# A softplus logarithm beside attention: from ScalarE's table to an eighteen-step polynomial on GpSimd

## The chip, the cores and the metric

The program runs on one core of a Trainium2 chip. The core has five instruction queues that run in order, each by itself: TensorE (PE in the profile; its weight loads are PEld), VectorE (DVE), ScalarE (ACT), GpSimd (POOL) and SyncE (SP, which here only issues DMAs). An instruction that waits for another engine holds up everything behind it in its own queue. The metric is device time in microseconds (us), the median of several executions; the profile is one further execution.

## The reference, cut to what matters

x has shape (4, 1024, 256) in float32: 4 batches of 1024 rows, 8 tiles of 128 rows each. One layer of three parts:

```python
x = x + attn_a(layernorm(x))      # 16 heads of 16, full softmax over 1024 keys, plus its own residual
x = x + ffn(layernorm(x))         # one 256x256 ternary weight
x = x + attn_b(layernorm(x))      # the memory: a recurrent fast-weight layer over the rows
x = x + ffn(layernorm(x))
```

The change lies in attn_b, in one of its three gates:

```python
alpha = (sigmoid(hidden @ aW.T + ab) * 0.1).mean(-1)
eta   = (sigmoid(hidden @ eW.T + eb) * 0.9 + 0.05).mean(-1)
theta = (softplus(hidden @ tW.T + tb) * 0.1).mean(-1)      # one number per row
```

For every chunk of 128 rows theta scales the gradient step of the fast weights; the chunks follow one another.

## The kernel before

**Attention.** The queries are cut into four blocks of 256 rows (BLOCKS, numbered k from 0 to 3). A unit is one block, one batch and half of the heads: 32 units. A unit runs over 8 tiles of keys and two pairs of heads, so 16 half-steps. A half-step (half) has TensorE compute the maxima scores of a later unit (mx, L244), the scores of this one (sc, L284 and L292) and, later, the weighted values (av, L312); VectorE reduces the maxima (nm, L249) and ScalarE takes the exponential of the scores (pt, L298, two instructions of 128x512 in a half-step). The scores live in three PSUM buffers.

**What runs beside it.** When a block's attention is through for a batch, finish (two row tiles at a time) adds the output projection, normalizes (hn), runs the feed-forward part, normalizes again (hd), transposes, and keeps hidden@tW.T+tb in xs. When a block is complete for all four batches, two calls of theta start, one for each chunk of 128 rows: chunks 0 and 1 in block 0, 2 and 3 in block 1, 4 and 5 in block 2, 6 and 7 in block 3. Then the memory of the chunk runs (prepare, advance, retrieve, output). Blocks 0 to 2 have their theta and memory beside the attention of the block that follows. Block 3 has no attention behind it: its chunks 6 and 7 are the tail, from about 1345 us on.

**theta before.** With x the 128x256 tile of xs (L505 to L515): VectorE makes u = min(-x, x); ScalarE u = exp(u) (L507); VectorE w = 1 + u (L509) and the rounding error u = (w - 1) - u (L510); ScalarE w = ln(w) (L512); GpSimd w = w - u (L513); VectorE w = max(x, 0) + w (L515). TensorE then takes the mean over the 64 features (thp, L521) and VectorE writes theta (thn, L525), which advance uses at L748. The exponential of the attention and the tanh of the memory share one of ScalarE's tables, the logarithm needs another one: the profile shows an ACT_TABLE_LOAD before the logarithm and one at the next exponential or tanh.

**The order.** The queues of PE, DVE and ACT are written out by hand, those of POOL and SP follow the order in which the program is recorded. A small planner interleaves the generators: each lane (settle, finish, theta, memory, outputs and so on) holds generators; "yield 1" means that the next piece of this generator comes no earlier than 1 unit of planner time later; a half-step is half a unit and the pieces' own TensorE work counts too (half, beside, piece). So a step of theta that changes its yields moves the pieces that come after it in all queues. The planner knows nothing of the time that POOL takes.

**POOL's other work.** The inverse square roots of all normalizations are a power on POOL: rsqrt (L72), then two small instructions in norm_stats (L84, L85) that make the bias; ScalarE applies them (L91, 128x256 for each row tile). In advance, the norm of the gradient goes through POOL too (n, L733), then wt on DVE (L748). prepare has several POOL copies and products (ms L591, xl L663, s1e to s2a L743, kl L548, qq L654).

```python
A.activation(dst[i], src[i], AF.Identity, scale=r[:, i : i + 1], bias=nb[:, i : i + 1])   # L91, hn and hd
```

Of the kernel before, what the change touches and what calls it, by code (L numbers as in the profile page):

```python
# [12 lines left out]
AF = mybir.ActivationFunctionType  # L13
ALU = mybir.AluOpType
# [12 lines left out]
D = 64  # L27
N5 = 512
EPS_LN = 1e-5

OWN = {mybir.EngineType.PE, mybir.EngineType.DVE, mybir.EngineType.Activation}


BLOCKS = ((0, 256), (256, 256), (512, 256), (768, 256))
# [3 lines left out]
def tile_hybrid(ctx: ExitStack, tc: tile.TileContext, x, ln_gamma, ln_beta, w_qkv, b_qkv, w_out, b_out,  # L38
# [3 lines left out]
    V, G, A = nc.vector, nc.gpsimd, nc.scalar  # L42
# [24 lines left out]
    def rsqrt(src, n, scale, eps, name):  # L67

        t = small.tile([P, 8], F32, tag="rs_in", name=f"rsi_{name}")
        r = small.tile([P, 8], F32, tag="rs_out", name=f"rso_{name}")  # L70
        V.tensor_scalar(t[:, :n], src, float(scale), float(eps), ALU.mult, ALU.add)  # L71
        G.tensor_tensor(out=r[:, :n], in0=t[:, :n], in1=nhalf[:, :n], op=ALU.pow)  # L72
        return r

    def norm_stats(src, n, name):
# [3 lines left out]
        for i in range(n):  # L79
            V.bn_stats(st[:, i, :], src[i])  # L80
            V.bn_aggr(mv[:, i, :], st[:, i, :])
        r = rsqrt(mv[:, :n, 1], n, 1.0, EPS_LN, name)
        nb = small.tile([P, 4], F32, tag="ln_nb", name=f"nb_{name}")
# [83 lines left out]
    def mps(shape, name, columns=256):  # L167

        taken[0] += columns
        return pools["m"].tile(shape, F32, tag="m", name=name)  # L170
# [325 lines left out]
    def theta(k, cs):  # L496


        xh = xs_of[k][:, cs].rearrange("p c b t -> p (c b t)")
        m = cs.stop - cs.start  # L500
        u, w = (
            pools["lp"].tile([P, N5 // 2], F32, tag=f"th{name}", name=f"{name}_{k}_{cs.start}")[:, : 2 * m * P]
            for name in "uw"
        )
        V.scalar_tensor_tensor(out=u, in0=xh, scalar=-1.0, in1=xh, op0=ALU.mult, op1=ALU.min)  # L505
        yield 1
        A.activation(u, u, AF.Exp)  # L507
        yield 1
        V.tensor_scalar(w, u, 1.0, None, ALU.add)  # L509
        V.scalar_tensor_tensor(out=u, in0=w, scalar=-1.0, in1=u, op0=ALU.add, op1=ALU.subtract)  # L510
        yield 1
        A.activation(w, w, AF.Ln)  # L512
        G.tensor_sub(w, w, u)  # L513
        yield 1
        V.scalar_tensor_tensor(out=w, in0=xh, scalar=0.0, in1=w, op0=ALU.max, op1=ALU.add)  # L515
        yield 2
        ps = mps([P, m, 2, 2], f"thp_{k}_{cs.start}", 256)
        for c in range(m):
            for b in range(2):
                o = (2 * c + b) * P  # L520
                T.matmul(ps[:, c, :, b], lhsT=w[:, o : o + P], rhs=ot, start=True, stop=True)  # L521


        c0 = BLOCKS[k][0] // P + cs.start
        V.tensor_scalar(thn[:, c0 : c0 + m, :], ps.rearrange("p c h b -> p c (h b)"), -0.01, None, ALU.mult)  # L525
        yield 1
# [466 lines left out]
    with ExitStack() as by_hand:  # L993
        by_hand.enter_context(tc.manual_schedule(engines=OWN))
        share(m=8)
        with ExitStack() as s1_:
# [105 lines left out]
            def input_stats(b):  # L1102
# [9 lines left out]

                V.tensor_scalar(r[:, 0, :], mv[:, :, 1], EPS_LN, None, ALU.add)
                G.tensor_tensor(out=r[:, 1, :], in0=r[:, 0, :], in1=nhalf, op=ALU.pow)
                G.tensor_mul(r[:, 2, :], r[:, 1, :], r[:, 1, :])
                G.tensor_mul(r[:, 2, :], r[:, 2, :], mv[:, :, 1])
                G.tensor_scalar(r[:, 2, :], r[:, 2, :], EPS_LN, None, ALU.add)
                G.tensor_tensor(out=r[:, 3, :], in0=r[:, 2, :], in1=nhalf, op=ALU.pow)
# [84 lines left out]
            def thetas(k, cs):  # L1203
                yield from theta(k, cs)
                for c in range(NT)[BLOCKS[k][0] // P :][cs]:
                    got[c]["theta"] = True
# [248 lines left out]
```

## Time and profile before

| what | value |
|---|---|
| median of 3 executions | 1477.69 us (1477.01 to 1477.88) |
| the profiled execution: time, span | 1477.84 us, 1476.1 us |
| granted TensorE clock, mean over the span | 0.929 |
| PE, DVE, ACT, POOL busy over the span | 92%, 69%, 53%, 16% |
| attention and what runs beside it, 250 to 1345 us | PE busy 1045.4 of 1095 us, clock 0.96 |
| tail, 1345 to 1476.1 us | PE busy 96.7 of 131.1 us, clock 0.78 |

How to read it: the page gives busy shares of the whole span; the table by stages cuts the span into windows; the timeline lists instructions in order of time, with the idle time of their engine ahead of them and what ended it in brackets. A name such as w<-w,u is output and inputs. The time outside the span (1.74 us in the profiled execution) is start and end.

### The profile page before, as it was taken

How to read it: one execution, taken by the hardware profiler on the slowest of the kernel's cores; microseconds unless marked ns; L12 is line 12 of the kernel's file. 1: busy time of each engine (PE TensorE's matmuls, PEld its weight loads, DVE VectorE, ACT ScalarE, POOL GpSimd, SP SyncE). 2: the span in 40 equal slices, each digit the busy share in tenths (PEclk: the TensorE clock that was granted, in tenths of full speed). 3: DMA queues.
4: the chain of work that ended last, by engine and by line, in shares of the span. 5: the costliest groups of instructions: out<-in, count | busy, mean ns of one | idle time of the engine just before them, and what ended most of it. 6: DMA issues, size and time to landing. Idle time of an engine off the chain costs nothing. (4 is left out here: it accounts for less than half of the span.)

```text
span 1476.1 us, 32993 instructions
## 1 busy us (share of the span) xinstructions
PE 1356.1 (92%) x13568; PEld 843.4 (57%) x13568; DVE 1020.5 (69%) x1640; ACT 785.9 (53%) x1477; POOL 236.8 (16%) x432
## 2 busy tenths in 40 slices
PE   6589999999999999999998999999999999996886
PEld 4346555556555556565654565666556656664664
DVE  5766767587777766877778767776778677712653
ACT  2124636466666555656566655655665555553333
POOL 4431111000000200211011101210102102201232
PEclk9759989999999789999999999999999899988877
DMA  6605432533333221222233222223232022101000
GB/s 219 203 32 197 142 135 81 199 103 109 106 101 112 81 60 59 65 76 84 90 101 109 76 84 77 86 77 98 77 126 80 17 76 90 49 23 37 22 8 29
DMA packets 98211, 132.71 MB, mean 90 GB/s; under 512 B 27980, under 2 KB 70284, under 8 KB 98060
## 3 DMA queue, kind: packets, MB, share of 16 engines
q1 hardware_dynamic: 97788, 129.81, 27.6%
q8 instruction: 107, 1.75, 0.5%
q10 hardware_dynamic: 272, 0.79, 0.1%
q14 instruction: 44, 0.36, 0.1%
HBM read 89.69 MB, written 38.76 MB: 87 GB/s over the span
## 5 line engine op out<-in xcount | busy, mean ns | idle before, releaser
L298 ACT ACTIVATE pt<-sc 128x512 f32<-128x512 f32 x1024 | 555.2, 594 | 452.2 <-PE sc L292 451.6
L249 DVE TENSOR_REDUCE nm<-mx 128x2 f32<-128x1024 f32 x512 | 617.8, 1220 | 144.1 <-PE mx L244 126.1
L284 PE MATMUL sc<-q0slot,kslot 32*128 32x256 f32 x2048 | 373.4, 339 | 24.2 <-ACT pt L298 12.8
L312 PE MATMUL av<-pt,v 128*32 128x256 f32 x4096 | 310.6, 404 | 6.9 <-DVE a L320 6.2
L284 PE MATMUL sc<-q1slot,kslot 32*128 32x256 f32 x2048 | 309.7, 291 | 0.0
L244 PE MATMUL mx<-kslot,q0slot 32*128 32x512 f32 x1024 | 264.8, 516 | 24.3 <-DVE lo L1160 14.0
L284 PEld LDWEIGHTS sc<-q0slot,kslot 32*128 32x128 f32 x2048 | 239.1, 191 | 51.0 <-ACT pt L298 25.4
L244 PEld LDWEIGHTS mx<-kslot,q0slot 32*128 32x128 f32 x1024 | 98.2, 189 | 241.0 <-issue 117.2
L292 PE MATMUL sc<-mslot,ones_r 32*128 32x512 f32 x1024 | 232.5, 405 | 1.8 <-DMA mslot<-d 1.8
L284 PEld LDWEIGHTS sc<-q1slot,kslot 32*128 32x128 f32 x2048 | 233.8, 193 | 0.0
L244 PE MATMUL mx<-kslot,q1slot 32*128 32x512 f32 x1024 | 217.0, 422 | 0.0
L312 PEld LDWEIGHTS av<-pt,v 128*32 128x32 f32 x4096 | 99.2, 111 | 126.9 <-issue 88.8
L292 PEld LDWEIGHTS sc<-mslot,ones_r 32*128 32x128 f32 x1024 | 124.1, 193 | 2.5 <-DMA mslot<-d 2.4
L244 PEld LDWEIGHTS mx<-kslot,q1slot 32*128 32x128 f32 x1024 | 101.2, 195 | 0.0
L1155 PE MATMUL cps<-hT,wg 128*128 128x512 f32 x128 | 61.4, 626 | 0.0
L1160 DVE SCALAR_TENSOR_TENSOR lo<-cps,bqk,hi 128x512 fp32r<-128x512 f32 x32 | 23.9, 751 | 53.4 <-ACT hi L1159 45.4
L1159 ACT ACTIVATE hi<-cps,bqk 128x512 fp32r<-128x512 f32 x32 | 22.0, 687 | 49.9 <-PE cps L1155 24.8
L72 POOL TENSOR_TENSOR rso_hn<-rsi_hn,nhalf 128x2 f32<-128x2 f32 (+1 forms) x17 | 12.0, 708 | 223.1 <-DVE rsi_hn L71 196.8
L72 POOL TENSOR_TENSOR rso_hd<-rsi_hd,nhalf 128x2 f32<-128x2 f32 (+1 forms) x17 | 12.0, 703 | 187.4 <-DVE rsi_hd L71 170.1
L893 PE MATMUL opf<-ffn,ohT 128*128 128x256 f32 x128 | 35.1, 422 | 6.6 <-ACT ohT L888 6.6
L1155 PEld LDWEIGHTS cps<-hT,wg 128*128 128x128 f32 x128 | 24.3, 200 | 28.8 <-issue 26.6
L1196 POOL TENSOR_SCALAR X<-X,rr_a 128x256 f32<-128x256 f32 x32 | 18.5, 588 | 124.4 <-DVE h L1138 124.4
(361 smaller groups left out, 1662.4 us busy)
## 6 DMA issues: line engine op xcount, KB each, us to landing
kslot<-dk SPq DMA_DIRECT2D x64, 512.0 KB
v<-dv SPq DMA_DIRECT2D x32, 604.0 KB
q1slot<-dq SPq DMA_DIRECT2D x128, 64.0 KB
q0slot<-dq SPq DMA_DIRECT2D x64, 128.0 KB
da<-a SPq DMA_DIRECT2D x31, 256.0 KB
dv<-vtile SPq DMA_DIRECT2D x8, 604.0 KB
X<-in_L_attn_a_x_dram SPq DMA_DIRECT2D x8, 512.0 KB
dq<-hi SPq DMA_DIRECT2D x16, 256.0 KB
```

The lines of the kernel that those rows point to most:

```text
L72: G.tensor_tensor(out=r[:, :n], in0=t[:, :n], in1=nhalf[:, :n], op=ALU.pow)
L244: T.matmul(ps[:, e, :], lhsT=qS[u][p][o : o + SL, j * P : (j + 1) * P], rhs=kt[o : o + SL, hf * N5 : (hf + 1) * N5], start=p == 0, stop=p ...
L249: V.tensor_reduce(nms[u][:, hf, 2 * pr : 2 * pr + 2, j], ps, AX.X, ALU.max, negate=True)
L284: T.matmul(ps[e][:, g * w : (g + 1) * w], lhsT=kS[u, g][o : o + SL, kc * P : (kc + 1) * P], rhs=qS[u][p][o : o + SL, g * w : (g + 1) * w], ...
L292: T.matmul(ps[e], lhsT=ones[o : o + SL, :], rhs=mslots[u % 2][o : o + SL, :], start=False, stop=True, skip_group_check=True,)
L298: A.activation(pt[:, e, :], ps[e], AF.Exp, scale=1.0 / HD**0.5)
L312: T.matmul(avs[u][SL * i : SL * (i + 1), part * w : (part + 1) * w], lhsT=v[:, kc, o : o + SL], rhs=pts[u, kc, i // 2][:, i % 2, part * w ...
L893: T.matmul(pf[:, e, :], lhsT=hT[:, cc, e, :], rhs=ffn[:, cc, :], start=cc == 0, stop=cc == 1)
L1155: T.matmul(ps, lhsT=wg[:, cc, n * P : (n + 1) * P], rhs=hT[:, cc, o], start=cc == 0, stop=cc == 1)
L1159: A.activation(high, ps, AF.Identity, bias=bqk[:, n : n + 1])
L1160: V.scalar_tensor_tensor(out=low, in0=ps, scalar=bqk[:, n : n + 1], in1=high.bitcast(F32), op0=ALU.add, op1=ALU.subtract,)
L1196: G.tensor_scalar(Xt, Xt, r[:, 6, t : t + 1], r[:, 7, t : t + 1], ALU.mult, ALU.add)
```

## The change

For blocks 0 to 2 (chunks 0 to 5) softplus' ln(1 + u), with u = exp(-|x|) between 0 and 1, is computed on POOL as a polynomial of degree 10 without a constant term, by Horner's rule, in eighteen instructions of 128x256. The two DVE instructions that split 1 + u, ScalarE's logarithm and POOL's subtraction go. The yields change with it: two pauses of 0.5 inside the polynomial and 1 after it. Block 3, whose theta lies in the tail, keeps the logarithm.

```diff
+LOG1P = (
+    1.0, -0.49999904, 0.33330004, -0.24954559, 0.19678117, -0.15311863, 0.10614265, -0.0570642, 0.01990716, -0.00325638
+)
@@ theta
         A.activation(u, u, AF.Exp)
         yield 1
-        V.tensor_scalar(w, u, 1.0, None, ALU.add)
-        V.scalar_tensor_tensor(out=u, in0=w, scalar=-1.0, in1=u, op0=ALU.add, op1=ALU.subtract)
-        yield 1
-        A.activation(w, w, AF.Ln)
-        G.tensor_sub(w, w, u)
-        yield 1
+        if k == len(BLOCKS) - 1:
+            V.tensor_scalar(w, u, 1.0, None, ALU.add)
+            V.scalar_tensor_tensor(out=u, in0=w, scalar=-1.0, in1=u, op0=ALU.add, op1=ALU.subtract)
+            yield 1
+            A.activation(w, w, AF.Ln)
+            G.tensor_sub(w, w, u)
+            yield 1
+        else:
+            G.tensor_scalar(w, u, LOG1P[-1], LOG1P[-2], ALU.mult, ALU.add)
+            for n, c in enumerate(LOG1P[-3::-1]):
+                G.tensor_mul(w, w, u)
+                G.tensor_scalar(w, w, c, None, ALU.add)
+                if n % 3 == 2:
+                    yield 0.5
+            G.tensor_mul(w, w, u)
+            yield 1
         V.scalar_tensor_tensor(out=w, in0=xh, scalar=0.0, in1=w, op0=ALU.max, op1=ALU.add)
```

In the order that results, POOL has the eighteen instructions in one stretch, but for two instructions of prepare (ms and the carry copy) in chunks 0, 2 and 4, and the power n of advance in the middle of chunks 3 and 5. From chunk 2 on the planner also sets the pieces of theta, memory and output at other half-steps than before on PE, DVE and ACT.

## The prediction

> **What bounds the kernel now.** First the table by stages, then half-clock stretches of it (columns: window; its length, then busy us and count of PE, PEld, DVE, ACT, POOL; granted clock; DMA share; GB/s).
>
> ```profile
> 250.00:1345.00 1095.00, 1045.39 (x11468) 649.40 (x11468) 782.73 (x1159) 649.75 (x1227) 130.72 (x249) 0.96 0.27 85
> ...
> 484.20:497.90 13.70, 13.65 (x115) 7.12 (x115) 11.06 (x21) 6.87 (x12) 3.72 (x9) 0.50 0.11 21
> ...
> 538.90:542.30 3.40, 3.40 (x32) 1.55 (x30) 3.33 (x9) 1.65 (x5) 0.53 (x1) 0.50 0.04 7
> ...
> 846.10:849.50 3.40, 3.40 (x27) 1.88 (x26) 2.44 (x6) 1.67 (x3) 0.65 (x2) 0.50 0.00 1
> ```
>
> Beside the attention PE is busy for 95%: it is the bound, and every us in which it idles is lost. The other three rows are the second loss: half clock, with PE fully busy. Then the groups by form, for what POOL pays (count | busy us, mean ns | idle before):
>
> ```profile
> L1196 POOL TENSOR_SCALAR X<-X,rr_a 128x256 f32<-128x256 f32 x32 | 18.5, 588 | 124.4 <-DVE h L1138 124.4
> ...
> L513 POOL TENSOR_TENSOR w<-w,u 128x256 f32<-128x256 f32 x8 | 5.9, 738 | 51.3 <-ACT w L512 51.3
> ```
>
> Third, ACT's timeline around the logarithm of chunk 1 (start, us; brackets: idle before):
>
> ```profile
> 517.47 0.42 ACT L507 ACTIVATE u<-u 128x256 f32<-128x256 f32 x1
> ...
> 528.82 1.09 ACT L91 ACTIVATE hd<-X,nb_hd,rso_hd 128x256 f32<-128x256 f32 x2
> ...
> 531.95 1.08 ACT L298 ACTIVATE pt<-sc 128x512 f32<-128x512 f32 x2 [0.51 <-PE sc L292]
> 533.05 1.28 ACT L512 ACT_TABLE_LOAD   x1
> 534.35 0.42 ACT L512 ACTIVATE w<-w 128x256 f32<-128x256 f32 x1
> 534.67 0.83 ACT L725 ACTIVATE sq<-dra 128x768 f32<-128x768 f32 x1
> 535.52 1.28 ACT L298 ACT_TABLE_LOAD   x1
> 536.81 1.09 ACT L298 ACTIVATE pt<-sc 128x512 f32<-128x512 f32 x2
> ```
>
> and the two engines on either side of it:
>
> ```profile
> 527.16 0.73 POOL L72 TENSOR_TENSOR rso_hd<-rsi_hd,nhalf 128x2 f32<-128x2 f32 x1 [14.05 <-DVE rsi_hd L71]
> 527.97 0.20 POOL L84 TENSOR_TENSOR nb_hd<-mv_hd,rso_hd 128x2 f32<-128x2 f32 x1
> 528.25 0.23 POOL L85 TENSOR_SCALAR nb_hd<-nb_hd 128x2 f32<-128x2 f32 x1
> ```
>
> ```profile
> 537.46 0.38 PE L284 MATMUL sc<-q0slot,kslot 32*128 32x256 f32 x1 [1.99 <-ACT pt L298]
> ```
>
> The reader is to see two things. The logarithm's two loads and itself (2.98 us) made pt 3.26 us late (536.81 against 533.55 by the 1.60 us spacing just before), and PE idled for 1.99 of them: 1.27 us of lateness are absorbed. And between u's exponential (517.89) and the normalization hd, which waits for POOL, lie four half-steps.
>
> **What goes.** PE's idle time that ended with the ACT row behind a logarithm: 1.24 us (chunk 0, at 484.25), 1.99 (1, at 537.46), 1.24 + 0.48 (2, at 796.28 and 799.16), 1.99 (3, at 845.42), 1.24 + 0.48 (4, at 1106.95 and 1109.83), 0.29 (5, at 1149.91): 8.95 us. Behind three of them the clock halves: 13.7, 3.4, 3.4 us. At half clock pt follows pt every 2.60 us (489.44 to 492.04), at full clock every 1.60 (800.10 to 801.70), so 38% of such a stretch is lost: 5.3 + 1.3 + 1.3 = 7.9 us. Bounds: 0, if these stretches have other causes, and 15.8, if the 6.8 us from 808.5 and the 13.7 us from 1146.4 belong here too; I take 7.9, the three that begin within 2 us of the idle. ACT's own 6 x 2.98 us and DVE's 6 x 0.73 us (L509, L510) are worth nothing beyond this: both engines have idle time in the half-steps (ACT 0.51 us in the row at 531.95).
>
> **What comes.** Eighteen POOL instructions in a chain: nine like L1196 (0.59), nine like L513 (0.74); a dependent one follows after 0.09 us (527.16 + 0.73 to 527.97: 0.08): 9 x 0.68 + 9 x 0.83 = 13.5 us. POOL is idle enough (131 of 1095 us), but its queue is in order.
>
> Chunks 0, 2, 4: behind the polynomial stand only prepare's xl and s1e to s2a, and DVE's L515. From exponential to L515 there were 19.6, 18.3 and 18.3 us; less 3 us for the logarithm that is gone, 15.3 remain, against 13.5 and 0.8 for ms and the carry. Cost 0; if the cover is short, L515 stands in DVE's queue ahead of the maxima.
>
> Chunks 1, 3, 5: behind the polynomial stand rso_hd and nb_hd, for which ACT waits at hd, with the next pt, so all scores, queued behind.
> - Chunk 1: 517.89 + 13.5 + the three small ones with gaps (527.16 to 528.48: 1.3) = 532.7. ACT came to hd at 528.93: 3.8 us late, less 1.27 absorbed: PE idles 2.5.
> - Chunk 3: in the new order n (1.03, and 0.09) stands after the eighth instruction; hd is again four half-steps behind the exponential. In the old trace those took 8.5 us in chunk 3 (828.27 to 836.76). So 13.5 + 1.1 + 1.3 = 15.9 against 8.5: 7.4 late, PE idles 6.1. n's inputs are there some 3 us after the exponential, so it adds no wait.
> - Chunk 5: the same queue and the same four half-steps: 6.1.
>
> Sum 14.7. Lower bound 9.7: chunks 3 and 5 with the 11.0 us that four half-steps took in chunk 1 (partly at half clock), 2.5 + 3.6 + 3.6. Upper bound 24: POOL 23% slower beside DVE, as al (774 ns) against kl (628), both L548, so 16.6 us for 13.5 in all three.
>
> Clock: each of the three waits is longer than those that halved it before. Price: the mean of the twelve half-clock stretches between 464 and 1345 us, 7.1 us x 38% = 2.7 each, 8.1 together; bounds 3 x 1.3 = 3.9 and 3 x 5.3 = 15.9. Sharing between DVE and POOL: L515 took 0.71 us at 800.85, while POOL worked on s2e, and 0.42 otherwise; PE waits for maxima only 9.1 us in the whole run, so I take +1.0, bounds 0 and 4.
>
> Moved: from chunk 2 on pieces change their half-steps; no instruction of PE, DVE or ACT is added by it, and SP's DMAs (au, el, dh, hid, out) change places by a few rows, no row of which PE waited for beside the attention except hid (0.6 us). At the end eight matmuls (gps, ops of chunk 5; each two records of 0.42 us, as opf has them on L893: 6.8 us) fall behind the attention into the tail, where PE idles 34 us; in return chunk 5's output chain is later and PE meets oth some 6 us later than at 1362.09, before vkps. I take -1.5; bounds -3.2 and +3.5.
>
> Sum: -8.95 - 7.9 + 14.7 + 8.1 + 1.0 - 1.5 = +5.5. Span 1476.1 + 5.5 = 1481.6; with 1.74 outside it 1483.3; the profiled execution was 0.15 above the median: **1483**.
>
> [...] From 533.5 on PE idled at most 1.99 us at a stretch and the clock still halved at 538.9; at 484.2 it stayed halved for 13.7 us with PE busy 13.65 of them. [...]
>
> [...]
>
> **The rivals.**
> - Faster, 1472. The polynomial is quicker than its rows, since L1196's mean holds disturbed ones (median 554) and gaps vanish: 9 x 0.55 + 9 x 0.72 = 11.5 us, 2 less in each chain: 0.5 + 4.1 + 4.1 = 8.7, and short drops (3.9): -8.95 - 7.9 + 8.7 + 3.9 - 1.5 = -5.8. With drops of 2.7 each it decides from 11.7 us downwards. For it: POOL's spans are rough. Against it: L513 is the very same form at 717 ns and more.
> - No change, 1478: lateness and gains cancel; the sum needs only 5.5 less, the size of one long half-clock stretch.
> - DVE waits at L515 too, 1498: with a polynomial of 16.6 us (the 23%) chunks 0, 2 and 4 are 2.1 us short, DVE's maxima stop, and PE follows (+6), while hd comes 3.1 us later still in the other three (+9).
> - Long half-clock stretches behind all three waits, 1491: 15.9 instead of 8.1.
>
> **How the numbers follow.** Two executions differ by less than 0.1%, so 0.2% (3 us) is what a measurement tells from no change: 1474.7 to 1480.7. Forecast 0.40, faster 0.28, no change 0.13, slow POOL 0.08, long stretches 0.11. Slower is 0.59, same 0.13, faster 0.28. The forecast's own range is 1480.7 to 1489; the range of 8 in 10 takes in the faster case, with 4 us below it for old clock losses above my 7.9, and the long stretches, and reaches the slow POOL's edge: 1468 to 1497.
>
> **What would show it.** Twelve table loads fewer (of those of L512, L298 and L686 four left, all in the tail) and no PE idle behind one before 1345 us. Eighteen POOL rows in 13.5 us six times. An ACT idle of 4 to 7 us before hd ended by nb_hd, and PE idle of 2.5 to 6 us, in chunks 1, 3 and 5; half clock behind them. Wrong if hd is ready in time, because the chain is shorter or the four half-steps longer, or if the clock stays whole.

## The result, and the profile after

The changed kernel takes 1535.95 us in the median of 6 runs (1533.05 to 1546.32), the kernel before 1477.79 us beside it (6 runs): a ratio of 1.0405, 95% interval 1.0375 to 1.0434. The direction was forecast, the size was not: +58 us for +5.5. The profiled execution took 1535.47 us, its span 1533.6.

All of it is lost beside the attention. The last exponential of the attention ends at 1403.9 us (before: 1345.4), and the tail behind it takes 129.7 us for 130.7. Cut at the same half-steps in both traces, the stretches are:

| stretch, us in the trace after | before | after | more |
|---|---|---|---|
| 459.8 to 551.9, chunks 0 and 1 | 88.5 | 92.1 | 3.6 |
| 551.9 to 781.2, no polynomial | 228.3 | 229.3 | 1.0 |
| 781.2 to 882.7, chunks 2 and 3 | 84.7 | 101.5 | 16.8 |
| 882.7 to 1118.3, no polynomial | 230.7 | 235.6 | 4.9 |
| 1118.3 to 1224.0, chunks 4 and 5 | 90.3 | 105.7 | 15.4 |
| 1224.0 to 1403.9, no polynomial | 163.3 | 179.9 | 16.6 |

The last row is the first surprise: no theta of blocks 0 to 2 runs there, and it loses as much as a pair of chunks does. The table by stages of the changed kernel (columns as in the prediction):

```profile
250.00:1403.90 1153.90, 1064.21 (x11452) 661.03 (x11444) 785.79 (x1145) 629.93 (x1198) 216.62 (x351) 0.92 0.26 80
...
526.55:540.20 13.65, 7.95 (x61) 5.34 (x63) 4.52 (x10) 5.07 (x9) 4.65 (x8) 0.50 0.00 0
854.25:867.90 13.65, 8.11 (x49) 5.75 (x53) 3.15 (x5) 4.60 (x9) 3.80 (x8) 0.50 0.01 4
...
1224.00:1403.90 179.90, 170.82 (x1612) 108.64 (x1610) 93.99 (x150) 92.38 (x177) 22.28 (x42) 0.85 0.16 49
```

Between 250 us and the end of the attention PE idles 89.7 us (before 49.6), and the granted clock falls from 0.96 to 0.92. The stretches of half clock behind the polynomials of chunks 1 and 3 last 13.65 us each; PE is busy for only 8 of them, since they begin inside a wait. In the last row PE is busy for 95% (before: 96%), so nearly all that it loses there is clock (0.85 for 0.95).

The groups by form, POOL:

```profile
L524 POOL TENSOR_SCALAR w<-w 128x256 f32<-128x256 f32 x48 | 42.2, 880 | 4.2
L523 POOL TENSOR_TENSOR w<-w,u 128x256 f32<-128x256 f32 x48 | 37.8, 787 | 3.8
L1210 POOL TENSOR_SCALAR X<-X,rr_a 128x256 f32<-128x256 f32 x32 | 18.5, 587 | 123.3 <-DVE h L1152 123.3
...
L521 POOL TENSOR_SCALAR w<-u 128x256 f32<-128x256 f32 x6 | 2.4, 405 | 30.3 <-ACT u L511 26.8 <-DMA hid<-dh 3.5
```

The products took what their row had promised (0.73 us in the median). The additions (L524) did not: 0.85 us, and 0.88 in the mean, for the 0.59 of the row they were priced by (L1196 before, L1210 here, which has two operators: X times a factor plus a summand, both from a tile). The first instruction, two operators in one, took 0.40.

POOL's timeline in chunk 1 gives the length of the chain:

```profile
514.11 0.40 POOL L521 TENSOR_SCALAR w<-u 128x256 f32<-128x256 f32 x1 [2.73 <-ACT u L511]
514.60 0.73 POOL L523 TENSOR_TENSOR w<-w,u 128x256 f32<-128x256 f32 x1
515.42 0.86 POOL L524 TENSOR_SCALAR w<-w 128x256 f32<-128x256 f32 x1
...
528.58 0.72 POOL L527 TENSOR_TENSOR w<-w,u 128x256 f32<-128x256 f32 x1
529.25 0.73 POOL L76 TENSOR_TENSOR rso_hd<-rsi_hd,nhalf 128x2 f32<-128x2 f32 x1
```

From 514.11 to 529.30: 15.2 us for 13.5. ACT's timeline shows what it holds up:

```profile
513.59 0.44 ACT L511 ACTIVATE u<-u 128x256 f32<-128x256 f32 x1
...
521.53 1.09 ACT L302 ACTIVATE pt<-sc 128x512 f32<-128x512 f32 x2 [0.81 <-PE sc L296]
530.63 1.09 ACT L95 ACTIVATE hd<-X,nb_hd,rso_hd 128x256 f32<-128x256 f32 x2 [8.01 <-POOL nb_hd L89]
531.62 1.06 ACT L302 ACTIVATE pt<-sc 128x512 f32<-128x512 f32 x2
```

hd comes to ACT at 522.62, 8.6 us after u's exponential (11 us in the trace before, part of that at half clock), and waits 8.01 us. PE, whose scores wait for pt, stands idle for most of that:

```profile
532.25 0.58 PE L288 MATMUL sc<-q0slot,kslot 32*128 32x256 f32 x1 [7.31 <-ACT pt L302]
```

In chunks 3 and 5 hd waits 9.02 and 9.04 us, and PE idles 8.57 us each time. PE's waits, in the whole run (us, times, longest):

```profile
PE sc L288 <- ACT pt L302: 32.7, 11, 8.6
PE mx L248 <- DVE nm L253: 16.9, 27, 1.5
...
PE sc L288 <- DVE kqm L667: 12.0, 4, 4.2
PE thp L535 <- DVE w L529: 5.1, 3, 1.8
PE vkps L573 <- DMA hid<-dh: 3.8, 2, 2.7
```

Before, these rows were 12.8, 9.1, 1.8, 0 and 0.6 us. The first row holds the wait that was forecast, larger. The fourth looks like a late polynomial, but VectorE has no idle time ahead of L529 (L515 before) in any of chunks 0 to 5; in chunk 3, for one:

```profile
876.06 0.42 DVE L529 SCALAR_TENSOR_TENSOR w<-xs,w 128x256 f32<-128x256 f32 x1
```

The new order sets L529 later in VectorE's queue, in chunks 1, 3 and 5 two or more half-steps nearer to thp than before (so pieces move in block 0 too, not only from chunk 2 on, as the section on the change has it). The run no_log below, which has that order and no work on POOL at this place, has the same wait:

```profile
PE thp L535 <- DVE u L529: 6.6, 3, 2.9
```

The third row was not forecast at all: the scores wait for kqm, a product of the memory (L667, in prepare), four times instead of once. PE's timeline in chunk 2 shows how, before and after the change:

```profile
806.49 0.61 PE L521 MATMUL thp<-ot,w 128*128 128x2 f32 x4
807.19 1.16 PE L651 MATMUL kqp<-qq,vk 64*128 64x128 f32 x8
808.27 0.61 PE L244 MATMUL mx<-kslot,q0slot 32*128 32x512 f32 x2
810.10 0.58 PE L284 MATMUL sc<-q0slot,kslot 32*128 32x256 f32 x2 [1.21 <-DVE thn L525]
```

```profile
810.11 1.16 PE L665 MATMUL kqp<-qq,vk 64*128 64x128 f32 x8
811.19 1.08 PE L698 MATMUL zT<-vk,s 64*64 64x128 f32 x8
812.21 0.50 PE L248 MATMUL mx<-kslot,q0slot 32*128 32x512 f32 x2
816.85 0.58 PE L288 MATMUL sc<-q0slot,kslot 32*128 32x256 f32 x1 [4.15 <-DVE kqm L667]
```

The scores and the memory's products draw on the same three PSUM buffers (pool m, three buffers; a half-step of scores takes two, kqp and zT one each). Before, the half-step held thp and kqp, and thn, which frees thp's buffer, takes 0.15 us (the scores wait 1.21). After, it holds kqp and zT: two memory products in one half-step, and the scores wait until kqm has read kqp. On DVE, in the trace after, kqm stands behind two scans and the maxima:

```profile
808.83 1.73 DVE L656 TENSOR_TENSOR_SCAN dzw<-m,ident 128x128 f32<-128x128 f32 x4
...
811.72 1.05 DVE L258 TENSOR_TENSOR nx<-nm 128x16 f32<-128x16 f32 x1
...
814.78 1.22 DVE L635 TENSOR_TENSOR_SCAN ms<-m,dzw 128x512 f32<-128x512 f32 x1
816.11 0.69 DVE L667 TENSOR_TENSOR kqm<-kqp,ms 128x512 f32<-128x512 f32 x1
```

In the new order kqp and zT meet in this way in chunks 2, 3, 4 and 5, in the old one in chunk 5 alone. That meeting is the "pair" of what follows. No polynomial takes part in it: it is the other half of the change, the yields. So there are two theories to be told apart. The queue theory: POOL's long chain and what stands behind it cost the 58 us. The order theory: the new yields do.

### The profile page after: what moved, and what is told of

It reads as the page before. It is cut to its first block, busy times and chain, and to the rows that moved or that the text cites. A ratio compares the mean times of both kernels' runs of the same rounds, so it can differ in the third digit from the quotient of the medians.

```text
span 1533.6 us, 33077 instructions
## 1 busy us (share of the span) xinstructions
PE 1369.7 (89%) x13568; PEld 852.3 (56%) x13568; DVE 1024.3 (67%) x1628; ACT 768.7 (50%) x1459; POOL 321.2 (21%) x534
## 4 chain that ended last, share of the span: by engine, by line
PE 66%; DVE 14%; ACT 7%; POOL 5%; DMA 4%; issue 3%; SPq 1%; DVEq 0%; ACTq 0%; POOLq 0%
PE av L316 14%; PE mx L248 11%; PE sc L288 9%; PE sc L296 7%; DVE nm L253 5%; PE cps L1169 3%; ACT pt L302 3%; PE opf L907 2%; PE vps L1192 2%; PE po L413 2%; PE pf L413 2%; POOL w L524 1%; PE gps L851 1%; POOL w L523 1%; PE vkps L573 1%
## 5 line engine op out<-in xcount | busy, mean ns | idle before, releaser
L316 PE MATMUL av<-pt,v 128*32 128x256 f32 x4096 | 315.5, 411 | 7.4 <-DVE a L324 7.4
L288 PE MATMUL sc<-q1slot,kslot 32*128 32x256 f32 x2048 | 314.0, 295 | 0.0
L248 PE MATMUL mx<-kslot,q0slot 32*128 32x512 f32 x1024 | 266.2, 520 | 31.1 <-DVE nm L253 16.9
L296 PE MATMUL sc<-mslot,ones_r 32*128 32x512 f32 x1024 | 235.8, 413 | 3.3 <-DMA mslot<-d 3.2
L288 PEld LDWEIGHTS sc<-q1slot,kslot 32*128 32x128 f32 x2048 | 237.4, 198 | 0.0
L1210 POOL TENSOR_SCALAR X<-X,rr_a 128x256 f32<-128x256 f32 x32 | 18.5, 587 | 123.3 <-DVE h L1152 123.3
L524 POOL TENSOR_SCALAR w<-w 128x256 f32<-128x256 f32 x48 | 42.2, 880 | 4.2
```

The lines of the kernel that those rows point to most:

```text
L248: T.matmul(ps[:, e, :], lhsT=qS[u][p][o : o + SL, j * P : (j + 1) * P], rhs=kt[o : o + SL, hf * N5 : (hf + 1) * N5], start=p == 0, stop=p ...
L288: T.matmul(ps[e][:, g * w : (g + 1) * w], lhsT=kS[u, g][o : o + SL, kc * P : (kc + 1) * P], rhs=qS[u][p][o : o + SL, g * w : (g + 1) * w], ...
L296: T.matmul(ps[e], lhsT=ones[o : o + SL, :], rhs=mslots[u % 2][o : o + SL, :], start=False, stop=True, skip_group_check=True,)
L316: T.matmul(avs[u][SL * i : SL * (i + 1), part * w : (part + 1) * w], lhsT=v[:, kc, o : o + SL], rhs=pts[u, kc, i // 2][:, i % 2, part * w ...
L524: G.tensor_scalar(w, w, c, None, ALU.add)
```

## Experiments: the order, the chain, and both

In all of them the line numbers are those of the changed kernel. The kernel before ran on the same chip each time; single times scatter by up to 1% about their median, so ratios with intervals carry the verdicts, and 1% is 14.8 us.

| kernel | median, us | ratio to before | 95% interval |
|---|---|---|---|
| ln_new_order | 1507.7 | 1.0202 | 1.0144 to 1.0260 |
| poly_old_order | 1495.1 | 1.0133 | 1.0075 to 1.0190 |
| no_log | 1491.6 | 1.0110 | 1.0067 to 1.0154 |
| poly_two_op | 1523.5 | 1.0316 | 1.0276 to 1.0357 |
| no_log_old | 1465.6 | 0.9914 | 0.9881 to 0.9946 |
| poly_even_old | 1476.1 | 0.9986 | 0.9955 to 1.0018 |
| poly_two_op_old | 1479.3 | 1.0022 | 0.9988 to 1.0055 |
| ln_new_apart | 1462.8 | 0.9918 | 0.9887 to 0.9949 |
| poly_apart | 1483.8 | 1.0052 | 1.0020 to 1.0084 |
| poly_short_apart | 1455.1 | 0.9857 | 0.9804 to 0.9909 |
| poly_short_old | 1467.2 | 0.9951 | 0.9911 to 0.9991 |
| ln_old_apart | 1477.8 | 0.9990 | 0.9950 to 1.0030 |
| poly_pool_rec | 1504.3 | 1.0188 | 1.0111 to 1.0265 |
| ln_pool_rec | 1476.7 | 1.0007 | 0.9972 to 1.0041 |
| poly_two_op_apart | 1471.0 | 0.9973 | 0.9940 to 1.0006 |

### Order and polynomial apart from each other

ln_new_order: the logarithm at the polynomial's yields (against the changed kernel).

```diff
-            G.tensor_scalar(w, u, LOG1P[-1], LOG1P[-2], ALU.mult, ALU.add)
...
-            G.tensor_mul(w, w, u)
+            V.tensor_scalar(w, u, 1.0, None, ALU.add)
+            V.scalar_tensor_tensor(out=u, in0=w, scalar=-1.0, in1=u, op0=ALU.add, op1=ALU.subtract)
+            yield 0.5
+            yield 0.5
+            A.activation(w, w, AF.Ln)
+            G.tensor_sub(w, w, u)
             yield 1
```

> The logarithm and its two VectorE instructions stand where the polynomial's yields put them (1, 0.5, 0.5, 1), so PE, DVE, ACT, POOL and SP have the changed kernel's order, with the logarithm in place of the polynomial. Queue theory (the loss comes from POOL's eighteen instructions and what waits behind them): 1474 to 1484 us, as before. Order theory (chunks 2 to 5 lose 32 us where chunks 0 and 1, whose order is unchanged, lost only 3.8, and 21.6 more are lost in stretches without a polynomial, so the moved pieces carry most of the 58): 1500 to 1525 us.

poly_old_order: the polynomial at the logarithm's yields.

```diff
             for n, c in enumerate(LOG1P[-3::-1]):
                 G.tensor_mul(w, w, u)
                 G.tensor_scalar(w, w, c, None, ALU.add)
-                if n % 3 == 2:
-                    yield 0.5
             G.tensor_mul(w, w, u)
             yield 1
+            yield 1
```

> The polynomial with the old yields (1, 1, 1), all eighteen instructions recorded at once: PE, DVE, ACT and SP have the old order and POOL too but for the polynomial. Queue theory: 1525 to 1540 us, ScalarE waiting 8 us for nb_hd in chunks 1, 3 and 5. Order theory: each pair of chunks loses what chunks 0 and 1 lost (3.8 us): 1478 + 11 = 1489, range 1484 to 1500.

no_log and no_log_old: neither of the two, at the new and at the old yields. They leave out the logarithm, so theta and the output are other numbers; only their time counts.

```diff
         else:
-            G.tensor_scalar(w, u, LOG1P[-1], LOG1P[-2], ALU.mult, ALU.add)
...
+            yield 0.5
+            yield 0.5
+            u, w = w, u
             yield 1
```

> Neither logarithm nor polynomial for chunks 0 to 5 in the changed kernel's order: theta is made from max(x, 0) + u, so the output is another. Queue theory: the logarithm's price comes back whole, 1478 - 9 (idle) - 8 (half clock) = 1461, range 1455 to 1470. Order theory: the moved pieces stay, 1483 to 1508. The difference to the changed kernel is what the eighteen POOL instructions cost in this order.

> Neither logarithm nor polynomial for chunks 0 to 5 (theta from max(x, 0) + u, another output), in the old order. If the logarithm's price is the same in both orders, 1477 - 16 = 1461 us (1507.7 - 1491.6 was its price in the new order; the prediction's two terms made 16.9). If the price of the new order were a mere effect of what the logarithm does to it, this would stand at 1470 or more. The difference to the polynomial in the old order (1495) is POOL's price without any change of order: 34 us if it comes out at 1461.

Measured: the new order costs 2.0% (29.8 us) with the logarithm, and about the same with neither of the two (1.0110 less 0.9914: 28.9 us). The polynomial in the old order costs 1.3% (19.6 us). The order theory has ln_new_order, poly_old_order and no_log in its ranges (1507.7, 1495.1, 1491.6), the queue theory none of the three. But the polynomial's 19.6 us in the old order, where its logarithm's price is already given back, are no small thing either: both theories are needed. The grid also gives the price of the logarithm, 0.86% (12.7 us) in the old order and 0.92% (13.6 us) in the new one, and that of the eighteen POOL instructions: 2.19% (32 us) in the old order, 2.95% (44 us) in the new one. By the intervals of the table each of these differences is good to about 0.3 to 0.7%.

The table by stages of ln_new_order, which has no polynomial, between 460 us and the end of the attention, and about one of the pairs of kqp and zT (PE ran them in the middle window):

```profile
460.00:1375.80 915.80, 859.28 (x9038) 539.04 (x9030) 628.22 (x956) 519.66 (x979) 126.51 (x229) 0.92 0.24 75
...
1268.30:1271.70 3.40, 3.09 (x31) 2.23 (x24) 3.40 (x4) 2.65 (x5) 2.38 (x4) 1.00 0.04 7
1271.70:1278.50 6.80, 5.27 (x42) 3.12 (x43) 3.75 (x5) 1.16 (x3) 0.88 (x3) 0.50 0.06 19
```

PE idles 56.5 us in the long row (before 43.6), 12.9 more, and is busy for 859.3 us (before 841.8), 17.5 more. The clock is 0.92 (before 0.95): 2 x 0.08 x 916 = 147 us at half clock for 2 x 0.05 x 885 = 89. So the larger part of the order's price is clock. Of the idle time, kqm has 6.3 us (before 1.8), w at thp 3.3 (0) and hid 2.3 (0.6). In the short rows PE was busy for 3.09 of 3.40 us with the pair and a half-step of attention, and the clock halved behind it.

### Is it that pair?

ln_new_apart: one yield of prepare, just behind kqp, is 0.5 from chunk 2 on, so that zT cannot come in the same half-step.

```diff
         g.update(au2=au2, ms=ms, kqm=kqm)
-        yield 0
+        yield 0.5 if c > 1 else 0
```

> The logarithm with the new yields (1507.7), but the last yield of prepare is 0.5 from chunk 2 on, so kqp (memory's scores) and zT (advance's first product) never fall into one half-step; in the new order they do in chunks 2, 3, 4 and 5, in the old one in chunk 5 alone. Theory (two memory pieces in one half-step take two of the three PSUM buffers, scores wait for kqm, and PE's window with the two pieces is followed by half clock): 1474 to 1484, the 30 us of the new order are gone. Rival (it is the later place of theta's or other pieces): 1498 to 1510.

Measured 0.9918: the 30 us of the new order are gone, and 12 more with them. Its row of the table by stages:

```profile
460.00:1339.70 879.70, 834.87 (x9054) 524.90 (x9051) 627.69 (x956) 521.97 (x983) 125.70 (x229) 0.95 0.25 78
```

PE idles 44.8 us, nearly as in the kernel before, the clock is back at 0.95, and PE's waits for kqm, 6.3 us in ln_new_order, are nil. Other pieces moved with this yield too, which may be why the time went below that of the kernel before; the pair is the part that was aimed at, not the only thing that differs.

poly_apart: the same line in the changed kernel.

> The changed kernel with one yield altered: the last of prepare is 0.5 from chunk 2 on, which keeps kqp and zT in different half-steps (all queues but POOL's polynomial as in ln_new_apart). Theory (the changed order costs through that pair, the same with polynomial or logarithm): 1536 - 45 = 1491 by the difference seen with the logarithm (1507.7 to 1462.8), range 1480 to 1495, with PE's waits for kqm gone (12.0 us in the changed kernel). Rival (the late polynomial hides the pair's price): 1515 or more.

Measured 1.0052 against 1.0405: one yield takes 52 us of the 58 away from the changed kernel, the polynomial untouched. The last stretch of the table above, 179.9 us in the changed kernel, takes 160.0 here (161.2 in ln_new_apart, 163.3 in the kernel before). PE's waits for kqm did not vanish, against the expectation; they are 3.5 us in two places, for 12.0 in four.

ln_old_apart: the same line in the kernel before, as a control.

> The kernel before with the one altered yield. It had kqp and zT in one half-step in chunk 5 alone: 1.8 us of waiting for kqm, and 6.8 us of half clock x 38% = 2.6 behind it. Pair theory: 1477 - 4.4 = 1472.5, range 1468 to 1476. Rival (what made the order of ln_new_apart quick, 1462.8, is something else that this yield brings): 1460 to 1466.

Measured 0.9990: no gain, against the expectation of 4.4 us. The pair of chunk 5 is only replaced: kqp now shares its half-step with an output product (ops), and PE waits 2.1 us for kqm instead of 1.8.

So the order is shown to be a cause, and this yield to mend it. That it is the pair is shown only in part, for the last stretch (from 1224.0 us in the changed kernel) speaks against it. The changed kernel has the pair of chunk 5 there, but the kernel before has it too, with the same wait for kqm (1.84 us) and the same half clock behind it. The first row is that of the kernel before, the other three are the half clock of the changed kernel in this stretch behind 1290 us:

```profile
1235.20:1242.00 6.80, 5.33 (x43) 3.19 (x44) 3.75 (x5) 1.23 (x3) 0.88 (x3) 0.50 0.07 19
```

```profile
1291.15:1297.95 6.80, 5.39 (x43) 3.25 (x44) 3.75 (x5) 1.29 (x3) 0.88 (x3) 0.50 0.06 19
1318.45:1332.15 13.70, 13.70 (x101) 8.53 (x94) 7.86 (x13) 3.74 (x8) 2.88 (x2) 0.50 0.10 34
1359.40:1386.70 27.30, 26.13 (x143) 16.10 (x143) 2.11 (x7) 11.24 (x22) 1.40 (x5) 0.50 0.06 21
```

What this stretch loses goes with the last two rows, which do not follow the pair: they begin just behind or within waits of 1.71 us (av, for DVE's a) and 2.05 us (sc, for pt). In the whole stretch the clock is halved for 54.6 us, for 17.1 in the kernel before and 17.1 in poly_apart. So the yield takes away more than the pair, and which of the moved pieces costs what there stays open. In ln_new_order, too, only 34 of the 150 us of half clock begin just behind a pair (7 of 85 in the kernel before).

### The length of the chain

poly_two_op: each addition with two operators, as the polynomial's first instruction has them. poly_two_op_old: the same in the old order.

```diff
-                G.tensor_scalar(w, w, c, None, ALU.add)
+                G.tensor_scalar(w, w, 1.0, c, ALU.mult, ALU.add)
```

> The eight additions are written as w times 1.0 plus c, two operators as in the polynomial's first instruction, which took 404 ns against 848 ns of the single addition. If the form sets the duration, the chain is 8 x 0.44 = 3.5 us shorter in each chunk: by the queue theory 1536 - 3 x 3.5 (idle) - some clock = 1515 to 1526; by the order theory under 5 us of gain, 1531 to 1536. If writing in place sets the duration (the first instruction reads u and writes w), the additions stay at 0.85 us and the time at 1533 to 1540.

> The additions with two operators (405 ns, as measured, for 848) in the old order: the chain is 3.5 us shorter, so hd's wait of 8 us falls to 4.5 in chunks 1, 3 and 5: 1495 - 10.6 = 1484.5, with less half clock 1480 to 1486. If the price is not that wait, 1490 to 1495.

The group of the additions in poly_two_op:

```profile
L524 POOL TENSOR_SCALAR w<-w 128x256 f32<-128x256 f32 x48 | 21.2, 442 | 4.0
```

442 ns in the mean and 405 in the median for 880 and 848: the form sets the duration, not that it writes in place. The gain is 0.89% (13 us) in the new order and 1.11% (16 us) in the old one, for 10.6 us of idle that were reckoned (in the traces PE idles 11.5 and 10.3 us less); what is beyond that lies within the intervals. Both are within or a little beyond what the queue theory expected, while the order theory expected under 5 us in the new order: the length of the chain does cost time.

poly_short_old: a polynomial of degree 6, ten instructions, with two-operator additions, in the old order.

```diff
-    1.0, -0.49999904, 0.33330004, -0.24954559, 0.19678117, -0.15311863, 0.10614265, -0.0570642, 0.01990716, -0.00325638
+    0.99990163, -0.49787487, 0.31764814, -0.19375911, 0.08556826, -0.0183383
...
-                G.tensor_scalar(w, w, c, None, ALU.add)
+                G.tensor_scalar(w, w, 1.0, c, ALU.mult, ALU.add)
```

> The same short polynomial (chain 6.5 us) in the old order, the third length after 17 us (1495) and 13.6 us (1479). Queue theory: hd no longer waits in chunks 1, 3 and 5, and the time comes down to that without a logarithm (1465.5) plus 1 to 4 us: 1466 to 1470. Rival (a fixed price for POOL in every chunk): 1473 to 1479.

Three lengths in one order: 15.2, 11.7 and 6.5 us of chain in chunk 1 give 1.0133, 1.0022 and 0.9951; without any it is 0.9914. (The expectations wrote 17 and 13.6 us for the first two, with ms and the gaps of chunk 0.) ACT's row at hd in chunk 1, in poly_old_order, poly_two_op_old and poly_short_old:

```profile
524.36 1.09 ACT L95 ACTIVATE hd<-X,nb_hd,rso_hd 128x256 f32<-128x256 f32 x2 [8.01 <-POOL nb_hd L89]
```

```profile
526.08 1.09 ACT L95 ACTIVATE hd<-X,nb_hd,rso_hd 128x256 f32<-128x256 f32 x2 [4.51 <-POOL nb_hd L89]
```

```profile
517.95 1.09 ACT L95 ACTIVATE hd<-X,nb_hd,rso_hd 128x256 f32<-128x256 f32 x2
```

The wait shrinks by the 3.5 us by which the chain does, and is nil at 6.5 us. In the old order chunk 5 has the same wait at hn (7.28 us in poly_old_order), whose power stands behind the polynomial there.

poly_even_old: the polynomial in chunks 0, 2 and 4 alone, the logarithm in the others.

```diff
-        if k == len(BLOCKS) - 1:
+        if k == len(BLOCKS) - 1 or cs.start:
```

> Polynomial for chunks 0, 2 and 4 alone, logarithm for 1, 3 and 5, old order. Theory of the queue (only hd in the odd chunks waits behind the polynomial): the even chunks give back half of the logarithm's price and cost nothing, 1477 - 8 = 1469, range 1464 to 1473, faster than before. Rival (the polynomial costs by sharing with VectorE, or by a late w, in every chunk alike: (1495 - 1461) / 6 = 5.7 us each): 1477 - 8 + 17 = 1486.

Measured 0.9986 (1476.1), between the two ranges: the even chunks do not cost what the odd ones do, but seem not to be free. If half of the logarithm's 12.7 us came back, the three polynomials cost about 4 us, an estimate that the intervals leave uncertain by about 5. PE's wait for the maxima, 9.1 us in the whole run before, is 16.0 here; how much of it comes from DVE instructions that take longer beside POOL (L515 in the trace before: 0.71 us at 800.85, 0.42 otherwise) was not separated.

### Another order on POOL

poly_pool_rec: POOL's queue, too, is written in the order of recording, old yields. ln_pool_rec: the same in the kernel before, as a control.

```diff
-OWN = {mybir.EngineType.PE, mybir.EngineType.DVE, mybir.EngineType.Activation}
+OWN = {mybir.EngineType.PE, mybir.EngineType.DVE, mybir.EngineType.Activation, mybir.EngineType.Pool}
```

> The polynomial of 18 with the old yields, and POOL's queue written in the order of recording like those of PE, DVE and ACT, which sets rso_hd and nb_hd ahead of the polynomial in chunks 1 and 3 and leaves them behind it in chunk 5. Queue theory: ScalarE's wait of 8 us for nb_hd is gone in chunks 1 and 3 and stands in chunk 5; the polynomial starts some 10.5 us later there, so w is about 5 us late and VectorE and PE wait for it at L529: against the logarithm with the same POOL order 5 to 15 us more, 1482 to 1492, less than 1495. Rival (the chain's length itself costs, wherever hd stands): 1492 to 1500, waits for nb_hd or not.

> The kernel before with POOL's queue in the order of recording, as control: 1470 to 1480, since no POOL instruction is long enough there to hold up hd.

This corrects a sentence of the section on the kernel before: POOL's queue does not simply follow the recording. Written so, rso_hd stands ahead of the polynomial in chunks 1 and 3, where it stood behind it. The control is unchanged (1.0007). The polynomial took 1.0188, not less than the 1.0133 of poly_old_order, so the expectation of 1482 to 1492 fell; its rival, 1492 to 1500, lies nearer. DVE's and then PE's timeline in chunks 1, 3 and 5:

```profile
530.41 0.42 DVE L529 SCALAR_TENSOR_TENSOR w<-xs,w 128x256 f32<-128x256 f32 x1 [4.20 <-POOL w L525]
849.07 0.42 DVE L529 SCALAR_TENSOR_TENSOR w<-xs,w 128x256 f32<-128x256 f32 x1 [5.54 <-POOL w L525]
1163.79 0.58 DVE L762 SCALAR_TENSOR_TENSOR wt<-n,thn 128x4 f32<-128x4 f32 x1 [9.24 <-POOL n L747]
```

```profile
1164.40 1.22 PE L781 MATMUL p<-s1a,j 128*128 128x256 f32 x2 [6.40 <-POOL s1a L757]
```

hd waits no more in chunks 1 and 3, as the queue theory said, nor does hn in chunk 5, where the wait was to stay. The wait for w that takes its place is 4.2 and 5.5 us on DVE, close to the 5 expected; in chunk 5 the power n, and with it wt and the states, stand behind the polynomial instead. So it is not hd as such: with a chain of 15 us, whatever is next in POOL's queue is late, and every one of the candidates (hd, hn, w, n) is on the way to PE.

### Both causes taken away

poly_two_op_apart: the change's polynomial of degree 10 with the two-operator additions and the altered yield. poly_short_apart: the short polynomial with the altered yield, its two yields behind the second and the fourth pair.

> The change's polynomial of degree 10 with the two mends, two-operator additions (13.6 us) and kqp apart from zT: 1484 less what the two operators saved in the old order (16) = 1468, range 1460 to 1472, so faster than the kernel before at single precision. Rival (the saving of two operators comes from the old order's places of hd): 1474 or more.

> As poly_apart, with a polynomial of degree 6 (error 1.4e-6 in the logarithm, so not to single precision) in ten instructions and two-operator additions: chain 0.41 + 4 x 1.31 + 0.82 = 6.5 us. Queue theory (what costs is what hd waits for): no wait is left, 1463 less the logarithm's 11 to 16 us plus some sharing = 1448 to 1456. Rival (POOL's work costs by sharing or by its share of time): 1460 to 1470.

Measured 0.9973 (1471.0) and 0.9857 (1455.1). The first is where the sum put it (1468, range to 1472), and its interval still holds 1. The second beats both kernels, by 1.4% and 5.3%, and, with intervals that just overlap, the logarithm with the same yield (0.9918) as well; its row of the table by stages:

```profile
460.00:1329.00 869.00, 822.47 (x9080) 518.52 (x9076) 628.27 (x945) 505.08 (x968) 158.42 (x283) 0.97 0.25 79
```

So the change's idea is worth having with a chain that fits its place and an order that keeps the pieces apart. The short polynomial's error of 1.4e-6 in the logarithm is the price.

## Why the prediction was wrong, step by step

| step | forecast, us | measured, us | from |
|---|---|---|---|
| logarithm gone (idle and clock) | -16.9 | -12.7 | no_log_old against before |
| chain, its waits, clock, sharing | +23.8 | +32 | poly_old_order against no_log_old |
| moved pieces and tail | -1.5 | +30 | ln_new_order against before |
| both together, beyond the sum | 0 | +10 (about -3 to +23) | rest |
| sum | +5.5 | +60 | ratio 1.0405 |

**The step that failed is "Moved".** It put -1.5, with bounds of -3.2 and +3.5, on the moved pieces, because no instruction of PE, DVE or ACT is added by them and because PE had waited for none of the moved DMAs but hid. It had no term for what the pieces do to each other in their new half-steps. The runs show +30: in ln_new_order PE idles 12.9 us more (for kqm, for w at thp and for hid), and the lower clock makes its work 17.5 us longer. The trace before had a row of this kind, the pair of chunk 5, with 1.8 us of waiting for kqm and half clock behind it. hid, counted at 0.6 us, is 3.8 in the trace after. The tail, which that step did look at, came out near the forecast: 129.7 us for 130.7.

**The chain: mechanism right, size too small.** The queue and the engine that waits (ACT at hd in chunks 1, 3 and 5) were right. Nine additions at 0.59 + 0.09 were the mis-sized term: one took 0.40, eight 0.85, which makes 15.2 us for 13.5. The reach of four half-steps was the second: 8.6 us in chunk 1 for 11, in part because the half clock of the old trace (511.5 to 521.8 us) was gone. The lateness that is absorbed was the third: 8.01 - 7.31 = 0.7 us in chunk 1 and 0.5 in the other two, for 1.27. PE idled 7.31, 8.57 and 8.57 us, 24.5 in all, for 2.5 + 6.1 + 6.1 = 14.7; that is just over the upper bound of 24.

**The cover of chunks 0, 2 and 4** held, but by luck. With ms, the carry copy and some slower instructions (in chunk 0 L523 up to 1.25 us, L524 up to 1.29) the polynomial took 17.8 us there in the trace after, where 15.3 were to cover 14.3. VectorE did not wait at L529, which the new order has moved back by two or more half-steps; in the old place, in poly_old_order, it waits 0.07 us, so the cover there is just used up.

**The clock.** Half clock did follow each of the three waits, for 13.65 us each, where 7.1 was taken; since they begin within the wait, 8 us of work were slowed in each: at 38%, 3 us, near the 2.7 forecast. Most of the time that the lower clock adds to PE's work has another reason, the order: PE is busy for 18.9 us more than before in the changed kernel, and for 17.5 us more in ln_new_order, which has no polynomial.

**The logarithm's price** was about right: 16.9 forecast, 12.7 and 13.6 measured, the interval of the first being 8 to 18. As forecast, of the loads behind logarithms only the tail's four are left (two before the logarithm, two before a tanh).

**The rivals.** The slow POOL (1498) came nearest in time, but not by its mechanism: VectorE waited for w in no chunk, and PE's 5.1 us at thp belong to the order. No rival put the price on the order. The faster rival's sum leaves out the 1.0 for sharing without a reason; with it, it is 1473.

The 10 us beyond the sum are the difference of three ratios and, by their intervals, not clear of zero. 2.7 us of it can be named: the power n between the instructions of the polynomial in chunks 3 and 5 (PE idle 8.57 for 7.32 and 7.17 in poly_old_order).

## What to carry to other kernels

When a change moves yields or pieces, read the new order for what now shares one slot (a half-step, a set of buffers), not only for what was added: an unchanged list of instructions cost 30 us here in another order, and one yield, meant to keep two products of the memory apart, gave it back. Price an instruction by a row with the same number of operators and the same kind of operands (constants or tiles), and not by name and shape alone: TENSOR_SCALAR on GpSimd at 128x256 took 0.40 us with two constants (L521), 0.85 with one (L524) and 0.59 with two operands from a tile (L1210). Compare a chain with the time to the next thing behind it in its queue: with 15.2, 11.7 and 6.5 us of polynomial in chunk 1, hd behind it waited 8.01, 4.51 and 0 us; with hd set ahead of the chain (poly_pool_rec), w was the late one, by 4.20 us.

## What was unexpected of the hardware

On GpSimd, adding a constant to 128x256 float32 took 848 ns in the median with one operator (L524 in the changed kernel) and 405 ns as "times 1.0, plus constant" with two (the same line in poly_two_op), in the same place, in and out of the same tile.

The clock halved behind windows in which PE hardly idled. In ln_new_order four stretches of half clock begin just behind kqp and zT; in the 3.4 us ahead of them PE had idled 0.50, 1.84, 0.68 and 0.36 us. Whether the half clock goes with the short idle or with the small matmuls themselves (64 rows, 64 or 128 columns) was not tried.
